# RNN lead of 52 steps instead of 64, set-up placed by RNN step, and eight matmuls without a result per RNN-only step

## The chip, the cores and the metric

The kernel runs on one core of a Trainium2 chip. The metric is the device time of one execution in microseconds (us). Five engines share the work: TensorE (PE, with its weight loads shown as PEld), VectorE (DVE), ScalarE (ACT), GpSimd (POOL) and SyncE (SP, which here only issues DMAs).

## The reference

A sequence of 4 batches, 1024 tokens and width 512 in float32 goes through four residual layers. Two of them are recurrences over the tokens, so that their steps can't run in parallel. The condition (4 x 512) is the start state of both, and the input of the last layer's small network.

```python
# layer 0: RNN, started from cond
h_t = tanh(x_t @ Wx + b + h_{t-1} @ Wh);           x1 = x + h
# layer 1: conv over 4 tokens (taps from cond), then a diagonal scan of 64 states
proj = conv(x1) @ Wp + bp;  B = softplus(proj[:64]);  C = tanh(proj[64:])
u = x1 @ Ws + bs;  s_t = decay * s_{t-1} + dt * B_t * u_t;  x2 = x1 + (C * s) @ Wo + bo
# layer 2: LSTM, started from cond, gates i, f, o, g
A = x2_t @ Wx + b + h_{t-1} @ Wh
c_t = sig(f) * c_{t-1} + sig(i) * tanh(g);  h_t = sig(o) * tanh(c_t);   x3 = x2 + h
# layer 3: per batch a 512 x 512 matrix, made once from cond
hid = gelu(layernorm(cond) @ w1 + b1);  a, b = split(hid @ w2 + b2)    # w2 is 512 x 8192
out = x3 + x3 @ (base + a @ b^T)
```

## The kernel before

**Passes and steps.** The tokens are cut into 32 chunks of 32 steps. The program is one list of steps, written out in full: `do_pass(c)` writes 32 of them, in which the LSTM works on chunk c and the RNN on a chunk that lies ahead. The RNN leads by two chunks: passes -2 and -1 (64 steps) have no LSTM in them and are the set-up phase, passes 0 to 29 have both, and passes 30 and 31 have the LSTM alone. Each engine executes its own instructions in the order in which the program writes them.

**One LSTM step.** TensorE runs 96 bf16 matmuls (`lstm_mm`, L360; h is split into three bf16 parts), in an order in which the four blocks of half A (gates of h units 0 to 255) end before the last block of half B. For each half, VectorE transposes the sums out of PSUM (L377), adds the parts and the input (L382), ScalarE takes tanh of the gates (L389), VectorE makes products (L393) and cell (L398), ScalarE tanh of the cell (L403), VectorE h (L406) and the two further splits of h (L187, twice). Then the next step's 96 matmuls can start. The RNN step beside it is 16 float32 matmuls (`rnn_mm`, L335), a transpose (L343), an addition (L344), both on VectorE, and a tanh on ScalarE (`rnn_h`, L347).

**Jobs.** All other work of a pass is a list of jobs, each with a slot (the step t of the pass) and a place in that step: "pe" (TensorE, between the LSTM's and the RNN's matmuls), "gap" (after half B's cell, before its tanh) or "end" (after `rnn_h`). Where several have one slot and place, they stand in the order of the list. The jobs are

- `project0` (L290, L304): the RNN's input of chunk c+3, four "pe" jobs;
- `ssm_jobs`: layer 1 of chunk c+1: x1 = x + h (L424), `taps` in four "pe" jobs and `skip` in one (L290, L457 to L472 for what follows), the scan (L475), a copy of the last state `s1` on ScalarE (L465), the product `y` on VectorE in place over the scan's result (L480), `out_mm` (L290) and `x2_end` (L492);
- `input_jobs`: the LSTM's input of chunk c+1 in four groups of 8 tokens: `input_mm` (L316, four "pe" jobs for each group), `input_turn` (L320, VectorE), `input_bias` (L328, ScalarE);
- `adapt_jobs`: layer 3 of chunk c-1: four additions (L666), four "pe" jobs (L673), a copy of 128x512 out of PSUM on ScalarE (L680), and DMAs to the output.

**Set-up.** The dictionary `early` holds what is done once, by pass and step: `split_wh2` (L274 to L279, 16 pieces; the LSTM's weights are split into three bf16 parts), `prepare_decay`, `fold_conv` (L255, L259), the layer norm (L526 to L547), `adapt_hidden` (L558), 32 `adapt_w2` (L575: 16 matmuls on 1/32 of w2, copies at L581, and the load of a further 512 KB of w2 into one of four buffers), `adapt_gather` (L589, POOL's DMAs), `adapt_sum` (L610), `base_identity` (L624) and 16 `adapt_layer` (L615 two matmuls, L616 an addition of 128x512). In this kernel all 32 `adapt_w2` stand in passes -1 and 0, one for each step from step 3 of pass -1, and the `adapt_layer` stand in pass 0. The identity `ident` is made on POOL, behind the DMAs that POOL issues at the start.

Of the kernel before, what the change touches and what calls it, by code (L numbers as in the profile page):

```python
# [20 lines left out]
TG = 8  # L21
CT = 32
# [15 lines left out]
def cond_resid_kernel(ctx: ExitStack, tc: tile.TileContext, a: dict, out: bass.AP):  # L38

# [135 lines left out]
    def load_late():  # L175
        quads(nc.sync, w1, a["w1"].rearrange("(j c q) n -> j q c n", j=4, c=KC))
        for j in range(W2_BUFS):
            load_w2(j)
        quads(nc.sync, base, a["base"].rearrange("(j c q) n -> j q c n", j=4, c=KC))
# [63 lines left out]
    def prepare_decay():  # L243
        for f in softplus_parts(sp, vec[:NS, 2:4], 2, "p"):
            f()
        nc.vector.tensor_mul(dec1, sp[:, 0:1], dt)
        nc.vector.tensor_scalar(dec1, dec1, -1.0, 1.0, ALU.mult, ALU.add)
        nc.vector.tensor_copy(decay, dec1.to_broadcast([NS, TC]))
# [12 lines left out]
    b2s = const.tile([P, 4, KC], F32, name="b2s", tag="b2s")  # L261

    def scale_b2():
        nc.vector.tensor_scalar(b2s[:, 0:3], b2[:, 0:3], 0.5, None, ALU.mult)
        nc.vector.tensor_copy(b2s[:, 3], b2[:, 3])

    def split_wh2(k, g):

        w, scale, cols = layer[:, k, g], 0.5 if g == 3 else 0.25, slice(g * D, (g + 1) * D)
        part = [x[:, k, cols] for x in wh2]  # L270
        left = xw2[1][:, 2 + g % 2].rearrange("p c t b -> p (c t b)")

        def first():
            nc.scalar.activation(part[0], upper(w), AF.Copy, scale=scale)  # L274
            nc.vector.scalar_tensor_tensor(left, w, scale, part[0], ALU.mult, ALU.subtract)

        def second():
            nc.scalar.copy(part[1], upper(left))
            nc.vector.tensor_tensor(part[2], left, part[1], ALU.subtract)  # L279

        return first, second
# [43 lines left out]
    def input_bias(c, n, g, m):  # L325

        x = xw2[c % 2][:, g, m, TG * n : TG * (n + 2), :]
        nc.scalar.activation(x, x, AF.Identity, bias=b2s[:, g, m : m + 1], scale=1.0 if g == 3 else 0.5)  # L328


    def rnn_mm(c, t):
        h = h0[c % 2] if t else h0[(c - 1) % 2]
        for k in range(KC):
            for j in range(4):
                nc.tensor.matmul(  # L335
                    acc0[CT * j : CT * j + B, :],
                    h[:, k, (t - 1) % TC, :], wh0[:, k, j * P : (j + 1) * P],
                    start=(k == 0), stop=(k == KC - 1),
                )

# [27 lines left out]
    class Half:  # L368
# [19 lines left out]
        def gates(self):  # L388
            nc.scalar.activation(self.gc[:, :4], self.gc[:, :4], AF.Tanh)  # L389
# [26 lines left out]
    def ssm_jobs(c):  # L416
# [3 lines left out]
        def sm(name):  # L420
            return small.tile([NS, TOK], F32, name=name, tag=name, bufs=1)

        jobs = [
            (m // 2, ("gap", "end")[m % 2], lambda m=m: v.tensor_add(x1[:, m, 3:, :], x[:, m], h[:, m]))  # L424
            for m in range(KC)
# [22 lines left out]
        jobs += [(1 + k, "pe", lambda k=k: taps(k)) for k in range(KC)]  # L448
        jobs.append((5, "pe", skip))

        def turn(n):
# [5 lines left out]
            (4, "end", lambda: act.activation(z, pb[:NS, 0, :], AF.Identity, bias=vec[:NS, 0:1])),  # L457
            (4, "end", lambda: act.activation(e, pb[:NS, 0, :], AF.Abs, bias=vec[:NS, 0:1])),
            (5, "end", lambda: act.activation(e, e, AF.Exp, scale=-1.0)),
            (5, "end", lambda: act.activation(u, e, AF.Copy, bias=2.0)),  # L460
            (6, "end", lambda: act.activation(cg, pb[NS:, 0, :], AF.Tanh, bias=vec[NS:, 0:1])),
            (7, "end", lambda: v.tensor_mul(u, u, e)),
            (7, "end", lambda: v.tensor_mul(w, u, u)),
            (7, "end", lambda: act.activation(p, w, AF.Copy, scale=2.0 * SERIES[-1])),
            (12, "end", lambda: act.copy(s1, y_last)),  # L465
# [17 lines left out]
        jobs += [(6 + n // 3, place(n), lambda n=n: turn(n)) for n in range(4)]  # L483
        jobs += [(8 + n // 3, place(n), f) for n, f in enumerate(chain)]
# [6 lines left out]
        def x2_end(m):  # L491
# [6 lines left out]
            (13, "pe", out_mm),  # L498
            *((13 + m // 2, "end", lambda m=m: x2_end(m)) for m in range(KC)),
            (14, "end", lambda: act.copy(x1[:, :, 0:3, :], x1[:, :, TC : TC + 3, :])),  # L500
# [4 lines left out]
    hid = prep.tile([P, KC, B], F32, name="hid", tag="hid")  # L505
# [45 lines left out]
    def adapt_hidden():  # L551
# [12 lines left out]
        nc.vector.tensor_add(hid, tt[:, :, :B], bm1.unsqueeze(2).to_broadcast([P, KC, B]))  # L564
        nc.scalar.activation(hid, hid, AF.Gelu)

    def adapt_w2(j):
# [4 lines left out]
        for k in range(KC):  # L572
            for t in range(4):
                n0 = P // 2 * (t % 2)
                nc.tensor.matmul(  # L575
                    ps[CT * t : CT * t + B, :], hid[:, k, :], w2[j][:, t // 2, k, n0 : n0 + P // 2],
                    start=(k == 0), stop=(k == KC - 1),
                )
        for t in range(4):
            copy = (nc.vector.tensor_copy, nc.scalar.copy)[t % 2]  # L580
            copy(xr[CT * t : CT * t + B, half, hd, rg], ps[CT * t : CT * t + B, :])  # L581
# [36 lines left out]
    def base_identity():  # L618
# [11 lines left out]
    early = {  # L630
        (-2, 9): [prepare_decay], (-2, 12): [scale_b2], (-2, 24): [fold_conv], (-2, 26): [adapt_center], (-2, 28): [adapt_norm],
        (-1, 2): [adapt_hidden], (-1, 20): [base_identity],
    }
# [3 lines left out]

    late = None
    for n in range(4 * KC):
        first, second = split_wh2((1, 0, 2, 3)[n // 4], n % 4)  # L640
        t = 4 + 3 * n // 2
        if late:
            at(-2, t, late)
        at(-2, t, first)
        late = second
    at(-2, 29, late)
    at(-2, 30, load_late)

    for half in range(2):
        at(-1, half, lambda half=half: adapt_bias(half))  # L650
        at(0, 7, lambda half=half: adapt_sum(half))
    for j in range(NW2):
        c, t = divmod(3 + j, TC)
        at(c - 1, t, lambda j=j: adapt_w2(j))
        if j % (NW2 // 2) == NW2 // 2 - 1:
            at(c - 1, t, lambda half=j // (NW2 // 2): adapt_gather(half))
    for n in range(B * KC):
        at(0, 8 + 3 * n // 2, lambda n=n: adapt_layer(n // KC, n % KC))


    def adapt_jobs(c, dst):
# [22 lines left out]
        jobs = [(2 + m, "end", lambda m=m: add(m)) for m in range(KC)]  # L684
        jobs += [(6 + k, "pe", lambda k=k: mm(k)) for k in range(KC)]
        return jobs + [(5 + KC, "end", end)]


    def input_jobs(c):
        jobs = []  # L690
        for n in range(TC // TG):

            ps = bank("proj2", [P, D], tag=("po", "ada")[n % 2], bufs=1)
            t = 15 + KC * n
            jobs += [(t + k, "pe", lambda n=n, k=k, ps=ps: input_mm(c, n, k, ps)) for k in range(KC)]
            jobs += [
                (t + KC - 1 + g // 2, "end", lambda n=n, g=g, ps=ps: input_turn(c, n, g, ps)) for g in (0, 2)
            ]
        jobs += [
            (23 + (KC * g + m) // 2, "end", lambda g=g, m=m: input_bias(c, 0, g, m))  # L700
            for g in range(4) for m in range(KC)
        ]
        return jobs

    def late_jobs(c):
        return [
            ((KC * g + m) // 2, "end", lambda g=g, m=m: input_bias(c, 2, g, m))
            for g in range(4) for m in range(KC)
        ]


    def do_pass(c, src=None, dst=None, lstm=True, rnn=True, ssm=True, late=True, last=False):

        jobs = []
        if dst is not None:
            jobs += adapt_jobs(c - 1, dst)
        if ssm:
            jobs += ssm_jobs(c + 1)
        if src is not None:
            jobs.append((2, "end", lambda: load_x(c + 4, src)))  # L720
        if rnn and c + 3 < NCHUNK:
            for m in range(KC):
                mm, end = project0(c + 3, m)
                t = ((0, 10, 11, 12) if lstm else (8, 10, 12, 14))[m]
                jobs += [(t, "pe", mm), (t, "end", end)]
        if ssm:
            jobs += input_jobs(c + 1)
        if late:
            jobs += late_jobs(c)
# [6 lines left out]
        for t in range(TC):  # L736
# [8 lines left out]
            if rnn:  # L745
                rnn_mm(c + 2, t)
# [16 lines left out]
            if lstm:  # L763
                if not (last and t == TC - 1):
# [6 lines left out]
            if rnn:  # L771
                rnn_pre(c + 2, t)
                rnn_h(c + 2, t)
            do(t, "end")
            for f in early.pop((c, t), ()) if dst is None else ():
# [7 lines left out]
    do_pass(-2, lstm=False, ssm=False, late=False)  # L783
    do_pass(-1, src=a["xT"][3], lstm=False, late=False)
    for m in range(2):
        lstm_input(0, 0, m)
    do_pass(0, src=a["xT"][4])
    assert not early
    prep_ctx.close()

# [3 lines left out]
    for c in range(1, NCHUNK):  # L794
        do_pass(
            c, src=a["xT"][c + 4] if c + 4 < NCHUNK else None, dst=dst(c - 1), rnn=c + 2 < NCHUNK,
            ssm=c + 1 < NCHUNK, last=c + 1 == NCHUNK,
        )
# [60 lines left out]
```

## Time and profile before

| | |
|---|---|
| median of 3 runs | 4811.99 us (4811.18 to 4814.89) |
| the profiled execution's own time | 4806.8 us |
| its span, first to last instruction | 4805.0 us |
| PE busy | 4609.9 us, 96% |
| DVE busy | 3816.7 us, 79% |
| ACT busy | 1749.1 us, 36% |
| first transpose of the RNN / of the LSTM | 18.6 us / 192.4 us from the span's start |

A row of the profile gives the line of the kernel, the engine, the operation with its operands and their shapes, how often it ran, the busy time, the mean of one, and what ended the idle time before it. Line numbers are those of the kernel before. In a timeline a row starts with its start and its length in us. PEclk is the clock that TensorE was granted, as a share of full speed.

### The profile page before, as it was taken

The page shows a single profiled execution, that of the slowest core. Times are in us where ns is not written, and L with a number is a line of the kernel's source. Part 1 is how long each engine was busy: PE and PEld are TensorE (multiplying, and loading weights), DVE is VectorE, ACT ScalarE, POOL GpSimd, SP SyncE. Part 2 cuts the span into 40 slices and gives each one's busy share as a digit, 9 for nine tenths or more (in the row PEclk, how much of TensorE's full clock was granted, in tenths as well). Part 3 has the DMA queues.
Part 4 walks back from the last instruction along what each step waited for, and adds up shares of the span by engine and source line. Part 5 has one row for each costly group of instructions (what it writes and reads, how often), then busy time and mean ns, then how long its engine had stood idle before and what let it go on. Part 6 is the DMA issues. An engine that isn't in the chain of part 4 may idle for free.

```text
span 4805.0 us, 321617 instructions
## 1 busy us (share of the span) xinstructions
PE 4609.9 (96%) x147040; PEld 3529.9 (73%) x147040; DVE 3816.7 (79%) x17843; ACT 1749.1 (36%) x8712; POOL 52.1 (1%) x95
## 2 busy tenths in 40 slices
PE   6899999999999999999999999999999999999876
PEld 4777777777777777777777777777777777777654
DVE  3678888888888888888888888888888878888776
ACT  2333333333333333333333333333333333333332
POOL 2100000000000000000000000000000000000000
PEclk7999999999999999999999999999999999999999
DMA  6400000000000000000000000000000000000000
GB/s 138 130 4 9 9 9 9 7 7 9 9 9 9 7 8 7 9 9 9 7 9 7 9 9 9 7 9 6 9 9 9 9 7 6 9 7 6 6 3 7
DMA packets 38787, 67.47 MB, mean 14 GB/s; under 512 B 9056, under 2 KB 26080, under 8 KB 36400
## 3 DMA queue, kind: packets, MB, share of 16 engines
q1 hardware_dynamic: 34064, 46.68, 3.8%
q8 instruction: 1149, 18.83, 1.7%
q14 instruction: 214, 1.75, 0.1%
q0 software_dynamic: 2208, 0.19, 0.1%
q10 hardware_dynamic: 1152, 0.01, 0.0%
HBM read 38.34 MB, written 8.39 MB: 10 GB/s over the span
## 4 chain that ended last, share of the span: by engine, by line
PE 94%; DVE 5%; issue 1%; ACT 0%; DMA 0%; ACTq 0%; DVEq 0%; SPq 0%
PE acc L360 58%; PE acc L335 18%; PE proj L316 9%; PE pb L290 3%; PE proj L290 2%; PE ada L673 2%; DVE tt L377 1%; DVE gc L382 1%; DVE h L187 1%; PE ssm_out L290 1%; DVE h L406 1%; DVE prod L393 0%; DVE gc L398 0%; PE pl L615 0%; PE pp L575 0%
## 5 line engine op out<-in xcount | busy, mean ns | idle before, releaser
L360 PE MATMUL acc<-wh,h 128*12 128x256 bf16 x98304 | 2875.0, 273 | 134.7 <-DVE h L187 130.0
L360 PEld LDWEIGHTS <-h 128*12 128x12 bf16 x98304 | 2266.7, 87 | 693.9 <-DVE h L187 372.3
L377 DVE STREAM_TRANSPOSE tt<-acc 128x256 f32<-128x256 f32 x2048 | 922.0, 450 | 425.5 <-PE acc L360 305.6
L335 PEld LDWEIGHTS acc<-wh,h 128*4 128x4 f32 x32768 | 815.6, 88 | 521.3 <-issue 212.2
L335 PE MATMUL acc<-wh,h 128*4 128x128 f32 x32768 | 1109.1, 276 | 31.6 <-ACT h L347 27.8
L389 ACT ACTIVATE gc<-gc 128x32 f32<-128x32 f32 x2048 | 469.7, 229 | 1038.6 <-DVE gc L382 948.4
L382 DVE TENSOR_REDUCE gc<-tt 128x32 f32<-128x128 f32 x2048 | 777.1, 379 | 35.3
L187 DVE TENSOR_TENSOR h<-h 128x8 f32<-128x8 f32 (+1 forms) x4098 | 681.1, 166 | 104.7
L403 ACT ACTIVATE th<-gc 128x8 f32<-128x8 f32 x2048 | 427.2, 209 | 831.9 <-DVE gc L398 831.9
L347 ACT ACTIVATE h<-pre 128x16 f32<-128x16 f32 x1024 | 221.4, 216 | 1144.7 <-DVE pre L344 1144.7
L316 PE MATMUL proj<-wx,x 128*32 128x512 f32 x4096 | 529.5, 592 | 2.6 <-issue 1.5
L406 DVE SCALAR_TENSOR_TENSOR h<-gc,th 128x8 f32<-128x8 f32 x2048 | 343.1, 168 | 221.8 <-ACT th L403 205.1
L343 DVE STREAM_TRANSPOSE tt<-acc 128x128 f32<-128x128 f32 x1024 | 316.2, 309 | 70.3 <-PE acc L335 70.1
L398 DVE SCALAR_TENSOR_TENSOR gc<-prod 128x8 f32<-128x8 f32 x2048 | 341.9, 167 | 35.5
L366 ACT COPY tt<-xw 128x32 f32<-128x32 f32 x2048 | 327.9, 207 | 0.0
L393 DVE SCALAR_TENSOR_TENSOR prod<-gc 128x16 f32<-128x16 f32 x2048 | 315.3, 154 | 0.0
L328 ACT ACTIVATE xw<-xw,b2s 128x64 f32<-128x64 f32 x1024 | 293.6, 334 | 0.4
L344 DVE TENSOR_TENSOR pre<-xw,tt 128x16 f32<-128x16 f32 x1024 | 179.8, 176 | 37.4
L290 PE MATMUL proj<-xin,wx 128*32 128x128 f32 x4096 | 138.8, 278 | 11.9 <-DMA wx<-in_Wx_dram 11.8
L290 PE MATMUL pb<-x,wp 128*32 128x128 f32 x4096 | 139.5, 274 | 0.1
L673 PE MATMUL ada<-layer,x 128*32 128x512 f32 x1024 | 131.6, 592 | 3.0 <-DVE x L666 3.0
L290 PEld LDWEIGHTS proj<-xin,wx 128*32 128x32 f32 x4096 | 117.1, 112 | 14.0 <-DMA wh<-in_Wh_dram 11.8
(116 smaller groups left out, 1179.0 us busy)
## 6 DMA issues: line engine op xcount, KB each, us to landing
layer<-in_w2T_dram SPq DMA_DIRECT2D x32, 512.0 KB, 4.1
xin<-in_xT_dram SPq DMA_DIRECT2D x128, 64.0 KB, 2.1
out_dram<-x SPq DMA_DIRECT2D x128, 64.0 KB, 1.8
layer<-in_Wh_dram SPq DMA_DIRECT2D x16, 256.0 KB, 9.7
wx<-in_Wx_dram SPq DMA_DIRECT2D x4, 1024.0 KB, 15.5
wx<-in_Wx_dram SPq DMA_DIRECT2D x4, 256.0 KB, 5.2
wh<-in_Wh_dram SPq DMA_DIRECT2D x4, 256.0 KB, 7.9
layer<-in_w_dram SPq DMA_DIRECT2D x4, 256.0 KB, 23.7
```

The costliest lines, as they stand in the source:

```text
L187: nc.vector.tensor_tensor(h[:, :, n], h[:, :, n - 1], upper(h[:, :, n - 1]), ALU.subtract)
L290: nc.tensor.matmul(dst[CT * j : CT * (j + 1)], columns(j), x, start=first, stop=final)
L316: nc.tensor.matmul(ps[CT * j : CT * (j + 1), :], tok, w[:, j], start=(k == 0), stop=(k == KC - 1))
L335: nc.tensor.matmul(acc0[CT * j : CT * j + B, :], h[:, k, (t - 1) % TC, :], wh0[:, k, j * P : (j + 1) * P], start=(k == 0), stop=(k == KC - 1),
L360: nc.tensor.matmul(acc2[mh][CT * j : CT * j + NP * B, :], parts, w[:, :, n0 : n0 + 2 * CT], start=(k == 0 and n == 0), stop=(k == KC - 1 a ...
L366: nc.scalar.copy(tt2[m][t % 2][:, :, :, :B], xw2[c % 2][:, :, 2 * m : 2 * m + 2, t, :])
L377: nc.vector.transpose(self.tt[:, :, :, B:].rearrange("p g c b -> p (g c) b"), acc2[self.m])
L382: nc.vector.tensor_reduce(self.gc[:, :4].rearrange("p g c b -> p (g c) b"), self.tt[:, :, :, : (1 + NP) * B].rearrange("p g c (s b) -> p ( ...
L389: nc.scalar.activation(self.gc[:, :4], self.gc[:, :4], AF.Tanh)
L398: nc.vector.scalar_tensor_tensor(self.c, self.prod[:, 1], 0.5, self.prod[:, 0], ALU.mult, ALU.add)
L403: nc.scalar.activation(self.th, self.c, AF.Tanh, scale=0.5)
L406: nc.vector.scalar_tensor_tensor(self.out[:, :, 0], self.gc[:, 2], 1.0, self.th, ALU.add, ALU.mult)
```

## The change

The RNN leads by `LEAD = 52` steps, so that the set-up phase has 52 RNN steps (20 in pass -2, 32 in pass -1), and the RNN ends at step 11 of pass 30. Layer 1 of a chunk therefore starts in slot 9 of the pass before it, and nearly every job moves to another slot. The LSTM's input of a chunk is made for 8 tokens in the pass before and for the other 24 in the pass itself. The input's bias moves from ScalarE (32 instructions of 128x64 in a pass) to VectorE (8 of 128x256); the factor 0.5 that went with it is now in the gates' tanh, and the g part of the weights and the bias is doubled in the set-up. The set-up is placed by RNN step (`at_step`); 12 of the 32 `adapt_w2` stand in it, and 20 in steps 0 to 19 of pass 0; the `adapt_layer` stand in steps 25 to 31 of pass 0 and 0 to 8 of pass 1. `adapt_w2` multiplies with 32 columns instead of 4 and needs one copy instead of four. In steps 0 to 24 of the passes without LSTM, `keep_busy` issues eight bf16 matmuls of 128x256 with `ident` as both operands, whose result nobody reads.

```diff
+LEAD = TC + 20
...
-    def input_bias(c, n, g, m):
-        x = xw2[c % 2][:, g, m, TG * n : TG * (n + 2), :]
-        nc.scalar.activation(x, x, AF.Identity, bias=b2s[:, g, m : m + 1], scale=1.0 if g == 3 else 0.5)
+    def input_bias(c, n, g):
+        x = xw2[c % 2][:, g : g + 2, :, TG * n : TG * (n + 1), :].rearrange("p g c t b -> p g c (t b)")
+        nc.vector.tensor_add(x, x, b2[:, g : g + 2].unsqueeze(3).to_broadcast([P, 2, KC, TG * B]))
...
+    bits = ident.bitcast(BF16)
+    idle = bank("idle", [P, 2 * P], tag="ada", bufs=1)
+    def keep_busy():
+        for n in range(2):
+            for j in range(4):
+                nc.tensor.matmul(idle[CT * j : CT * (j + 1), :], bits[:, :CT], bits, start=True, stop=True)
...
-            (m // 2, ("gap", "end")[m % 2], lambda m=m: v.tensor_add(x1[:, m, 3:, :], x[:, m], h[:, m]))
-            for m in range(KC)
+            (9, "end", lambda: add(slice(0, 2), 0, TC - 4)),
+            (10, "gap", lambda: add(slice(2, 4), 0, TC - 4)),
+            (11, "end", lambda: add(slice(0, 4), TC - 4, TC)),
...
-        jobs += [(1 + k, "pe", lambda k=k: taps(k)) for k in range(KC)]
-        jobs.append((5, "pe", skip))
+        jobs += [(12 + k, "pe", lambda k=k: taps(k)) for k in range(KC)]
+        jobs.append((16, "pe", skip))
...
-            (12, "end", lambda: act.copy(s1, y_last)),
+            (23, "end", lambda: act.copy(s1, y_last)),
...
-        jobs += [(8 + n // 3, place(n), f) for n, f in enumerate(chain)]
+        jobs += [(19 + n // 3, place(n), f) for n, f in enumerate(chain)]
...
-            (13, "pe", out_mm),
-            *((13 + m // 2, "end", lambda m=m: x2_end(m)) for m in range(KC)),
+            (24, "pe", out_mm),
+            *((24 + (m + 1) // 2, ("end", "gap")[m % 2], lambda m=m: x2_end(m)) for m in range(KC)),
...
-        for t in range(4):
-            copy = (nc.vector.tensor_copy, nc.scalar.copy)[t % 2]
-            copy(xr[CT * t : CT * t + B, half, hd, rg], ps[CT * t : CT * t + B, :])
+        nc.scalar.copy(xr[:, half, hd, rg], ps)
...
+    def at_step(i, f):
+        c, t = divmod(i - LEAD, TC)
+        at(c, t, f)
+    for n, f in enumerate(decay_parts()):
+        at_step(1 + n // 2, f)
...
+            at_step(5 + n, first)
...
+    at_step(10, load_w1)
+    for j in range(W2_BUFS):
+        at_step((14, 18)[j // 2], lambda j=j: load_w2(j))
+    at_step(21, load_base)
+    at_step(20, fold_conv)
...
+    at_step(24, adapt_center)
+    at_step(25, adapt_norm)
...
+    at_step(30, adapt_hidden)
+    NPRE = 12
     for j in range(NW2):
...
+        if j < NPRE:
+            at_step(32 + 3 * j // 2, f)
+        else:
+            at(0, j - NPRE, f)
...
+    for half in range(2):
+        at(0, 24, lambda half=half: adapt_sum(half))
+    at(0, 23, base_identity)
     for n in range(B * KC):
-        at(0, 8 + 3 * n // 2, lambda n=n: adapt_layer(n // KC, n % KC))
+        c, t = divmod(25 + n, TC)
+        at(c, t, lambda n=n: adapt_layer(n % B, n // B))
...
-        jobs = [(2 + m, "end", lambda m=m: add(m)) for m in range(KC)]
-        jobs += [(6 + k, "pe", lambda k=k: mm(k)) for k in range(KC)]
-        return jobs + [(5 + KC, "end", end)]
+        jobs = [((1, 2, 5, 6)[m], "end", lambda m=m: add(m)) for m in range(KC)]
+        jobs += [((16, 21, 22, 23)[k], "pe", lambda k=k: mm(k)) for k in range(KC)]
+        return jobs + [(23, "end", end)]
...
+    def input_jobs(c, n, t):
...
+        last = t + KC - 1
+        return [(t + k, "pe", lambda k=k: mm(k)) for k in range(KC)] + [
+            (last, "end", lambda: input_turn(c, n, 0, ps[0])),
+            (last + 1, "gap", lambda: input_turn(c, n, 2, ps[0])),
+            (last + 1, "end", lambda: input_bias(c, n, 0)),
+            (last + 2, "gap", lambda: input_bias(c, n, 2)),
+        ]
...
+        if -1 <= c < NCHUNK - 1:
+            jobs += ssm_jobs(c + 1)
+            jobs += input_jobs(c + 1, 0, 25)
         if src is not None:
-            jobs.append((2, "end", lambda: load_x(c + 4, src)))
+            jobs.append((12, "end", lambda: load_x(c + 4, src)))
+        if c + 3 < NCHUNK:
             for m in range(KC):
                 mm, end = project0(c + 3, m)
+                jobs += [(17 + m, "pe", mm), (17 + m, "end", end)]
+        if lstm:
+            for n in range(1, TC // TG):
+                jobs += input_jobs(c, n, KC * (n - 1))
...
             if rnn:
-                rnn_mm(c + 2, t)
+                rnn_mm(*r)
+            if not lstm and t < 25:
+                keep_busy()
```

## The prediction

> **What bounds the kernel now.** I read the busy time and clock in stretches first, then the timeline of single steps, then the waits, and the chain of waits for what ended each step. The stretches (length, busy time and instructions of each engine, clock, DMA share, GB/s) are two of the set-up and one of the passes with LSTM and RNN:
>
> ```profile
> 57.00:84.00 27.00, 18.79 (x320) 10.12 (x320) 13.38 (x32) 9.57 (x25) 0.00 (x0) 0.50 0.72 177
> 150.00:190.00 40.00, 36.77 (x1183) 26.35 (x1187) 18.93 (x88) 14.18 (x66) 9.09 (x16) 1.00 0.67 216
> 2000.00:2143.00 143.00, 141.34 (x4560) 108.53 (x4560) 117.18 (x551) 53.43 (x269) 0.00 (x0) 1.00 0.03 8
> ```
>
> From 57 to 112 us the clock is halved. There an RNN step takes 2.78 us (in the chain its matmuls start at 59.92, 62.71, 65.49, each 1.93 long); the first RNN steps, at full clock, took 2.02. The LSTM's first matmul comes at 190.5 us, so the set-up is 4% of the time.
>
> One LSTM step, and the start of the next, in pass 14 (timeline, rows of other work left out):
>
> ```profile
> 2273.40 2.79 PE L360 MATMUL acc<-wh,h 128*12 128x256 bf16 x96
> ...
> 2274.57 0.18 DVE L344 TENSOR_TENSOR pre<-xw,tt 128x16 f32<-128x16 f32 x1
> ...
> 2275.26 0.45 DVE L377 STREAM_TRANSPOSE tt<-acc 128x256 f32<-128x256 f32 x1
> ...
> 2276.02 1.05 PE L290 MATMUL proj<-xin,wx 128*32 128x128 f32 x32
> ...
> 2276.89 1.05 PE L335 MATMUL acc<-wh,h 128*4 128x128 f32 x32
> ...
> 2277.86 2.36 PE L360 MATMUL acc<-wh,h 128*12 128x256 bf16 x80
> ...
> 2279.25 0.22 ACT L347 ACTIVATE h<-pre 128x16 f32<-128x16 f32 x1 [1.07 <-DVE pre L344]
> 2279.37 0.18 ACT L465 COPY s<-w 64x4 f32<-64x4 f32 x1
> ...
> 2279.58 0.34 DVE L480 SCALAR_TENSOR_TENSOR w<-w,sp,cg 64x128 f32<-64x128 f32 x1 [0.37 <-ACT s L465]
> 2279.85 0.43 DVE L377 STREAM_TRANSPOSE tt<-acc 128x256 f32<-128x256 f32 x1
> ```
>
> From start to start TensorE spends 2.62 us on the LSTM, 0.87 on one "pe" job and 0.97 on the RNN (0.87 where nothing holds it, as in the set-up): 4.46 a step. In pass 31, without RNN and without most jobs, transposes are 4.45 apart too. So a step has **two limits of nearly one length**: the recurrence through DVE and ACT at 4.455, and PE with one job at 2.62+0.86+0.87 = 4.35. Half A's transpose starts 1.87 us after the first matmul. What VectorE still does then delays it: in slot 12's "end" job `y` waits 0.37 for ScalarE's copy of `s1`, the transpose comes 1.99 after its matmuls, and that step takes 4.61 in the median pass. Slots 15 to 31 are at 4.45 to 4.47. Passes 1 to 31 lie 22 us in all over 31 x 142.56, pass 0 lies 20 over.
>
> Three prices for later. `skip` (0.77 from start to start) and an `adapt_jobs` matmul group (0.85), in the order of PE alone:
>
> ```profile
> 3101.99 0.93 PE L290 MATMUL pb<-x,ws 128*32 128x128 f32 x14
> ...
> 3106.45 1.03 PE L673 MATMUL ada<-layer,x 128*32 128x512 f32 x8
> 3107.30 0.94 PE L335 MATMUL acc<-wh,h 128*4 128x128 f32 x28
> ```
>
> And POOL's making of `ident`, held up behind the small loads on its queue:
>
> ```profile
> 32.31 0.29 POOL masks.py:199 TENSOR_SCALAR_AFFINE_SELECT ident<-ident 128x128 f32<-128x128 f32 x1
> ```
>
> **What the Trainium skill says.** "TensorE: Matmul & The Clock Gate", Part 1, has a clock that activity raises to full and that falls to half after an idle window of about 3.4 us. The two values agree (1.00 and 0.50), the condition doesn't: here it fell at 29.9 us after six RNN steps with no matmul gap over 0.97 us, so a low share is enough. Its section on the 16 sub-arrays says that ScalarE and VectorE work strictly in order and that TensorE only pulls weight loads ahead; the 0.37 us wait above is such a case. "VectorE: DVE Perf Modes", on Mode 2×_2P, keeps fp32 tensor_tensor at one element per cycle, 0.96 GHz: 1.04 ns. The trace: 287 ns for 128x128 (L424), 176 for 128x16 (L344), so 0.99 ns.
>
> **The change, part by part.**
>
> *Set-up.* (a) `keep_busy` stands behind the first `rnn_mm` and needs `ident`, ready at 32.6 us. PE's queue is stopped from 18.5 to 32.6, and the second RNN step, at 19.5 before, starts at about 33: **13.5 us lost**. (b) Eight such matmuls cost 8/96 of 2.62 = 0.22 us, in the 1.1 us in which PE waits for tanh: nothing on the path while that cover lasts. Worth of the clock: at half clock, three groups of 32 matmuls in a window of 6.8 us brought it back (43.6 to 50.4), 2.5 (RNN alone) didn't; with 0.44 us more each I take it back at 43.6. (c) Steps: 1 to 4 at 2.78, to 44; 5 to 20 with a split each, bound by VectorE (0.69+0.69 and the waits for two ACT copies of 0.6): 2.52 warm, 2.78 cold; steps 13 to 19 have no `keep_busy` and turn cold: to 83. 20 to 31: 2.05 to 2.8 each, with `fold_conv`, layer norm, hidden layer and their table loads (1.28 each) some 8 us more: to 117. 32 to 44: RNN 0.87 and a PE remainder of 0.22+0.87+0.45 (`adapt_w2`) in two steps of three: 2.3 each, to 147. 45 to 51: 2.1, to 162. The LSTM starts at about 163 instead of 190.5: **-27**. Always warm: 154 (-36); cold to step 31: 178 (-12).
>
> *DMA and queues.* SP's order stays (x, weights, w1, w2, base), and 4 x 512 KB in six steps (14 us, 150 GB/s) is under the 216 seen. POOL gets one memset more, after `ident`. No gain or loss here.
>
> *Passes 0 and 1.* 20 `adapt_w2` of 0.45 beside a full step: 2.62+0.86+0.87+0.45 = 4.80, +0.35 each: 7. Their 16 loads of w2 disturb PE's instruction fetch: the 28 loads of before cost about 7 us of "issue" in the set-up, so 4 (0 to 10). `base_identity` (16 x 0.12) and `adapt_sum` (2 x 0.6) before transposes: 3. `adapt_layer` 1.05 in 13 full slots and three free ones: 13.7+1. Sum 29, against about 21 before: **+8** (3 to 18).
>
> *Steady passes.* Three collisions, each against 4.455:
> - Slot 16 has `skip` and an `adapt_jobs` group: 2.62+0.85+0.77+0.87 = 5.11, **+0.66**. The RNN's tanh and everything in the next step wait behind it.
> - Slot 23 "end": in ACT's order the 128x512 copy (0.585, about 0.49 to the next start) now stands before the copy of `s1`. `y` then starts 2.20 after the matmuls instead of 1.72, and the transpose at 2.49: **+0.50** on what it costs now.
> - Slot 11 "end": the addition of the last four tokens needs the tanh of the same step. The tanh ends 1.60 after the matmuls, the addition takes 0.22, the `input_turn` behind it 0.37 to the next start: transpose at 2.15, **+0.28**.
>
> Elsewhere: `input_bias` on VectorE, 0.287+128x0.00099 = 0.41 (0.35 to the next start), and `input_turn` (0.37) in "gap", where VectorE has 0.36 before half B's h: +0.01 each, below which nothing is seen; if full lengths count, 0.1 in nine slots. ScalarE's 293.6 us of bias were idle-time work: nothing. `out_mm`'s long step is hidden behind slot 23: -0.07. Loads of x move to slot 12 with their fetch stalls, and the outputs to a step with slack: -0.1. Sum 1.27 a pass; 29 passes have slots 16 and 23 with RNN: **+37** (22 to 58).
>
> *Sum.* -27+8+37 = **+18** on 4806.8. The median of the runs shown lies 5.2 above this execution: 4812+18 = **4830**.
>
> **Rivals.** (A) As summed, 4830: 0.44. (B) The clock stays low through the set-up: -12 instead of -27, 4845; for it, that a PE 70% busy (18.79 of 27.00) was left at half clock: 0.16. (C) The gap doesn't hold turn and bias: nine slots of 0.1 in 29 passes, +26, 4856; against it, reciprocals of 0.32 cost nothing in "gap": 0.12. (D) Faster: the collisions vanish because queues run apart enough to absorb them, so that only -27+8 is left: 4793. It decides where the three collisions together cost under 0.3 a pass (9 us). Against it, 0.12 us at the transpose is already visible in slot 12: 0.12. (E) Both halves cancel, with the set-up at -36 and the collisions at two thirds (+25): 4809; also where `keep_busy` isn't stopped by `ident`: 0.16.
>
> **Numbers.** A measurement here can tell 0.2% (9.6 us) from no change. Slower is A, B, C: 0.72; same E: 0.16; faster D: 0.12. The range leaves out D and the outer half of C: 4803 to 4857.
>
> **What would show it.** Right: PE idle from 18.5 to 32.6 with the wait on POOL; LSTM from about 163 us; steps of 5.1 in slot 16; `y` waiting about 0.85 behind ACT; a full clock from about 44 us with a dip. Wrong: steps near 4.46 in slots 11, 16 and 23, an LSTM start after 175 or before 152, or transposes late in slots 4, 8 and 12.

## The result and the profile after

The changed kernel takes 4839.9 us (median of 5 runs, 4838.52 to 4843.03), the kernel before 4811.99 (4811.18 to 4814.89): a ratio of 1.0063, interval 1.0051 to 1.0075. It is slower by 27.9 us, three times what can be told from no change. The profiled execution of after has 4843.03 us with a span of 4841.2; against the 4805.0 of before that is 36.2 more, 8 more than the medians differ, because the execution of before was 5.2 below its median and the one of after 3.1 above.

I cut both spans into stretches (us); the first ends with the LSTM's first matmul, and a pass is counted from its first transpose of half A to that of the next pass:

| stretch | before | after | difference | predicted |
|---|---|---|---|---|
| start to the LSTM's first matmul | 190.5 | 176.0 | -14.5 | -27 |
| passes 0 and 1 | 162.9 + 144.7 | 172.0 + 154.4 | +18.8 | +8, and +1.3 of pass 1's collisions |
| passes 2 to 30 | 4154.7 | 4185.4 | +30.7 | +36 |
| pass 31 and tail | 150.3 | 150.3 | 0 | 0 |

(The LSTM's first transpose comes 1.9 us after its first matmul in before and 3.1 in after, where the clock is halved from 175.1 to 178.6 us; this is the 1.2 us that the rows leave.) All three signs are those of the prediction; each size is off.

**Stretches of after** (length, busy time and instructions of PE, PEld, DVE, ACT, POOL, clock, DMA share, GB/s):

```profile
57.00:84.00 27.00, 14.28 (x328) 9.09 (x320) 16.14 (x41) 11.64 (x29) 0.00 (x0) 0.79 0.55 140
...
2000.00:2143.00 143.00, 140.28 (x4529) 108.82 (x4525) 117.97 (x555) 45.57 (x236) 0.00 (x0) 1.00 0.03 8
```

The clock of the first stretch rose from 0.50 to 0.79, but in the same 27 us the number of matmuls hardly changed (320 to 328), of which some now have no result. In the steady stretch PE is busy 1.06 us less of 143 and does 31 matmuls fewer: it waits. ACT's busy time fell by 7.9 us and shortened nothing.

**The start of after's set-up** (timeline, rows of PE and the row of POOL that ends the wait):

```profile
30.82 0.29 POOL masks.py:199 TENSOR_SCALAR_AFFINE_SELECT ident<-ident 128x128 f32<-128x128 f32 x1
31.17 0.62 PE L350 MATMUL idle<-ident 128*32 128x256 bf16 x8 [13.50 <-POOL ident masks.py:199]
...
42.09 0.52 PE L292 MATMUL proj<-xin,wx 128*32 128x128 f32 x10 [1.43 <-issue]
...
51.58 1.71 PE L292 MATMUL proj<-xin,wx 128*32 128x128 f32 x26 [5.56 <-issue]
...
60.79 0.28 PE L337 MATMUL acc<-wh,h 128*4 128x128 f32 x2 [3.54 <-issue]
```

The bracket is the idle time ahead of a row and what ended it. The first wait is the predicted one: 13.50 us for `ident`. The other three, 10.5 us in all, end with "issue": no semaphore that the profile shows held PE, and the prediction had none of them here (before has 2.1 us of them on PE between 17 and 110 us).

The DMA packets of the trace show what ends these waits. The profile calls two of its DMA queues "instruction"; a packet of 16 KB on one of them ended at 40.63, 49.94 and 59.33 us, and PE went on at 42.09, 51.58 and 60.79, each time 1.5 to 1.6 us later. In pass 0 of the twelve traces here (about 40 such packets each), all 148 "issue" waits of PE end 1.1 to 1.7 us after one. By these times, what PE waits for is its instructions.

**Slot 16 of after** in pass 14, with `skip` and an `adapt_jobs` group between the LSTM's matmuls and the RNN's:

```profile
2307.81 2.80 PE L371 MATMUL acc<-wh,h 128*12 128x256 bf16 x96
...
2310.43 1.03 PE L711 MATMUL ada<-layer,x 128*32 128x512 f32 x8
2311.29 0.93 PE L292 MATMUL pb<-x,ws 128*32 128x128 f32 x14
2312.07 1.03 PE L337 MATMUL acc<-wh,h 128*4 128x128 f32 x28
2312.83 0.28 PE L371 MATMUL acc<-wh,h 128*12 128x256 bf16 x2
...
2314.90 0.45 DVE L388 STREAM_TRANSPOSE tt<-acc 128x256 f32<-128x256 f32 x1 [1.09 <-PE acc L371]
```

From 2307.81 to 2312.83 are 5.02 us, also the median over the passes; slot 17 takes 4.66. PE goes from group to group without a gap, and VectorE waits 1.09 us for it. The first two matmuls of slot 17 are recorded ahead of the RNN's last, so that the sum of the two steps, 9.68 (8.91 in before), is surer than its split.

**Slot 23 of after** in pass 14 (the answer to the step shown of before, where this stood in slot 12):

```profile
2344.39 2.79 PE L371 MATMUL acc<-wh,h 128*12 128x256 bf16 x96
...
2345.94 0.59 ACT L718 COPY x<-ada 128x512 f32<-128x512 f32 x1
...
2346.42 0.19 ACT L482 COPY s<-w 64x4 f32<-64x4 f32 x1
...
2346.64 0.34 DVE L497 SCALAR_TENSOR_TENSOR w<-w,sp,cg 64x128 f32<-64x128 f32 x1 [0.90 <-ACT s L482]
2346.91 0.43 DVE L388 STREAM_TRANSPOSE tt<-acc 128x256 f32<-128x256 f32 x1
...
2349.32 2.80 PE L371 MATMUL acc<-wh,h 128*12 128x256 bf16 x96
```

The copy of 128x512 stands ahead of the copy of `s1` on ScalarE, `y` waits 0.90 instead of 0.37, the transpose starts 2.52 us after the matmuls, and the step, which is step 24, takes 4.93.

### The profile page after: what moved, and what is told of

It reads as the page before. It is cut to its first block, busy times and chain, and to the rows that moved or that the text cites. A ratio compares the mean times of both kernels' runs of the same rounds, so it can differ in the third digit from the quotient of the medians.

```text
span 4841.2 us, 321327 instructions
## 1 busy us (share of the span) xinstructions
PE 4615.9 (95%) x147344; PEld 3550.6 (73%) x147344; DVE 3865.2 (80%) x18001; ACT 1495.0 (31%) x7661; POOL 52.6 (1%) x96
## 4 chain that ended last, share of the span: by engine, by line
PE 89%; DVE 8%; issue 1%; ACT 1%; DMA 0%; POOL 0%; ACTq 0%; DVEq 0%; POOLq 0%
PE acc L371 56%; PE acc L337 16%; PE proj L318 9%; PE pb L292 3%; PE proj L292 2%; DVE tt L388 2%; PE ada L711 2%; DVE gc L393 1%; DVE h L191 1%; DVE h L417 1%; DVE prod L404 1%; DVE gc L409 1%; DVE tt L354 0%; ACT x L718 0%; PE pl L633 0%
## 5 line engine op out<-in xcount | busy, mean ns | idle before, releaser
L318 PEld LDWEIGHTS proj<-wx,x 128*32 128x32 f32 x4096 | 118.2, 110 | 6.0 <-PE pp L595 0.6
```

Of the source, the lines that this page charges most:

```text
L318: nc.tensor.matmul(ps[CT * j : CT * (j + 1), :], tok, w[:, j], start=(k == 0), stop=(k == KC - 1))
```

## Experiments

The theory: three separate costs (slot 16, slot 23, `ident` ahead of the second RNN step) and a dearer pass 0 make the result, and a gain from the shorter set-up stands against them. The rivals: the queues absorb the collisions; the matmuls without a result, and not the stop, decide the set-up; the loads of w2, and not the added PE work, decide pass 0. Ratios are to the kernel before on the same chip. The start of the LSTM is good to some 6 us only: four kernels with one and the same set-up (after, E1, E2, E5; "the four equals" below) have it at 176.0, 172.6, 175.0 and 170.2. Pass 0 varies too: in five kernels with one and the same program for it (after, E2, E3, E8, E4) it takes 172.0, 170.6, 171.1, 171.9 and 166.6. Of E4's difference 1.7 us are the clock's, as shown below.

**E1, `skip` alone in its slot.**

```diff
-        jobs.append((16, "pe", skip))
+        jobs.append((17, "pe", skip))
...
-                jobs += [(17 + m, "pe", mm), (17 + m, "end", end)]
+                t = (18, 19, 20, 29)[m]
+                jobs += [(t, "pe", mm), (t, "end", end)]
```

> The changed kernel with skip in slot 17, alone on TensorE there, and project0 in slots 18, 19, 20 and 29 instead of 17 to 20. Nothing else moves. If the two TensorE jobs in slot 16 are the cost, slot 16 (5.02 us in the median pass) and slot 17 (4.66) both go back to 4.46, which is 29 times 0.66 to 0.78: 19 to 23 us less than the changed kernel's 4840, so about 4819. If those steps are long because of the loads of x that slot 12 now starts and PE's instruction fetch beside them, the time stays within 5 us of 4840.

Measured: 4812.19 us, ratio 1.0006 (0.9999 to 1.0013), level with before. In pass 14, on PE:

```profile
2294.10 1.03 PE L711 MATMUL ada<-layer,x 128*32 128x512 f32 x8
2294.96 1.05 PE L337 MATMUL acc<-wh,h 128*4 128x128 f32 x32
2295.93 2.79 PE L371 MATMUL acc<-wh,h 128*12 128x256 bf16 x96
2298.55 0.93 PE L292 MATMUL pb<-x,ws 128*32 128x128 f32 x14
```

The two groups now stand in two steps, and slots 16 and 17 take 4.46 in the median, against 5.02 and 4.66. Passes 2 to 30 are 22.0 us shorter; 28 x (0.57+0.21) is 21.8 (pass 30 has no RNN in these slots). So the one step with two "pe" jobs is most of the loss of the steady passes, and the queues absorb none of it. The other 7 us of the spans' difference lie in the set-up (3.4, inside the spread named above) and mostly in passes 0 and 1.

**E2, the copy of `s1` ahead of the copy of 128x512.**

```diff
-        return jobs + [(23, "end", end)]
+        return jobs + [(24, "end", end)]
```

> The changed kernel with layer 3's copy out of PSUM and its output DMAs in slot 24 instead of 23, so that ScalarE copies s1 first. If the copy ahead of s1 is what makes the step after slot 23 last 4.93 us, y waits 0.37 us again instead of 0.85 and that step takes 4.60: 29 times 0.33, 9 to 10 us less, about 4830. If out_mm on TensorE holds that step anyway, under 3 us are gained.

Measured: 4825.25 us, 1.0036 (1.0023 to 1.0049); passes 2 to 30 are 13.2 us shorter. Pass 14:

```profile
2334.45 2.79 PE L371 MATMUL acc<-wh,h 128*12 128x256 bf16 x96
...
2336.16 0.34 DVE L497 SCALAR_TENSOR_TENSOR w<-w,sp,cg 64x128 f32<-64x128 f32 x1 [0.37 <-ACT s L482]
2336.43 0.43 DVE L388 STREAM_TRANSPOSE tt<-acc 128x256 f32<-128x256 f32 x1
2337.17 1.08 PE L292 MATMUL ssm_out<-w,wo 64*32 64x128 f32 x32
2338.18 1.06 PE L337 MATMUL acc<-wh,h 128*4 128x128 f32 x32
2339.05 2.80 PE L371 MATMUL acc<-wh,h 128*12 128x256 bf16 x96
```

The wait of `y` is 0.37 again and the step takes 4.60, as before. So ScalarE's order is the cause: 4.93-4.61, 28 times, is 9.0 us. Of the other 4, 3 lie in slot 16, which the edit doesn't touch: its mean was 5.14 in after and 5.04 here, by steps in which PE waits longer for "issue". The lines show more: PE goes from one group to the next without a gap (2.72 to `out_mm`, 1.01 for it, 0.87 for the RNN, 4.60 in all). What makes this step long is `out_mm`, not the transpose at 1.98.

**E3, no `keep_busy`.**

```diff
-            if not lstm and t < 25:
-                keep_busy()
```

> The changed kernel without the matmuls that have no result. If the stop for the identity is the larger part, the second RNN step starts at about 19.5 us instead of 31.6, the clock stays low for more steps, and the LSTM starts at 158 to 165 us instead of 176: 4822 to 4829. If the clock that they hold is worth what the stop costs, the LSTM starts near 176 and the time stays at 4836 to 4844. If it is worth more, it is later and slower than 4844.

Measured: 4823.36 us, 1.0029 (1.0017 to 1.0041), faster than after. The LSTM starts at 161.9, the second RNN step at 19.6 instead of 31.6, where it now waits for the first step's tanh alone:

```profile
19.61 1.06 PE L337 MATMUL acc<-wh,h 128*4 128x128 f32 x32 [0.96 <-ACT h L358]
```

Until 110 us the clock is halved for 65 us in all, most of it from 48 to 102.

**E4, `keep_busy` with an operand that is there.** The bf16 parts are taken from a weight tile instead of from `ident`.

```diff
-    bits = ident.bitcast(BF16)
+    bits = upper(wx0[:, 0])[:, : 2 * P]
```

> The changed kernel with the upper halves of the RNN's first input weights as the operands of the matmuls without a result; these have landed before the first RNN step, so that nothing waits for the identity. If the stop and the clock are separate effects, the LSTM starts 13 us earlier than in the changed kernel, at 163 us, and the time is about 4827, below that of the kernel without these matmuls. If the instruction fetch stalls between 40 and 61 us are what holds the early steps, they come at the same time and the gain is under 5 us.

Measured: 4823.53 us, 1.0027 (1.0015 to 1.0038); the LSTM starts at 158.8, and the clock is halved for 41 us in all, most of it from 56 to 83. The second RNN step with its matmuls without a result:

```profile
18.74 1.06 PE L337 MATMUL acc<-wh,h 128*4 128x128 f32 x32 [0.73 <-ACT h L358]
19.61 0.41 PE L350 MATMUL idle<-wx 128*32 128x256 bf16 x8
```

The stop is gone, and the LSTM starts 11 to 17 us earlier than in the four equals, about what the stop was worth. Against E3 the clock is full for 24 us more, the LSTM starts 3 us earlier, which is within the spread, and the medians are equal. So in the set-up `keep_busy` costs through its operand, and its use for the clock is 3 us or less.

**E5, no late loads of w2.** The last 16 loads are left out (the last 16 `adapt_w2` read the same four buffers again).

```diff
-            load_w2(j + W2_BUFS)
+            if j + W2_BUFS < 16:
+                load_w2(j + W2_BUFS)
+            else:
+                w2[j + W2_BUFS] = w2[j]
```

> The changed kernel without the last 16 of the 32 loads of w2, which are those issued in pass 0; the matmuls on them run on what lies in the buffers, so layer 3's matrix is left out in part. All matmuls and copies stay. If the loads disturb PE's instruction fetch, pass 0 (172.0 us in the changed kernel) loses 8 to 14 us and the time is near 4829. If the 20 groups of matmuls in full steps are the whole cost of that pass, it loses under 3.

Measured: 4832.38 us, 1.0057 (1.0040 to 1.0074); pass 0 is 167.3 instead of 172.0. PE's waits in pass 0, in us, times and longest: first after, then this kernel.

```profile
PE acc L371 <- issue: 3.9, 7, 0.7
PE pp L595 <- issue: 3.8, 6, 0.9
...
```

```profile
PE acc L371 <- issue: 3.6, 7, 0.7
PE pp L595 <- issue: 0.7, 1, 0.7
```

What the loads cost isn't settled. Pass 0 is 4.7 us shorter than in after and 3.3 shorter than in E2, but E4, which has all the loads, has 166.6, or 168.3 with the clock's 1.7 us. The "issue" waits fall to 4.3 us from after's 8.6 (which holds 0.9 on `skip`'s and `taps`' line); the other kernels with all the loads have 4.6 to 8.4. One execution of each kernel can't tell this from the spread, and the ratio is after's within the intervals. What is shown is that waits of 4.3 us stay without these loads, so that they are not the only cause, and that the 8 to 14 us of the first theory are not there.

**E6, 20 of the 32 `adapt_w2` in the set-up.**

```diff
-    NPRE = 12
+    NPRE = 20
...
-            at_step(32 + 3 * j // 2, f)
+            at_step(32 + j, f)
...
-            at(0, j - NPRE, lambda half=j // (NW2 // 2): adapt_gather(half))
+            f = lambda half=j // (NW2 // 2): adapt_gather(half)
+            at_step(32 + j, f) if j < NPRE else at(0, j - NPRE, f)
```

> The changed kernel with 20 of the 32 pieces of w2 in the set-up, one for each RNN step from step 32, and 12 in pass 0 instead of 20. If a piece costs pass 0 the 0.35 us of its matmuls and 0.5 us or so of fetch stalls, pass 0 gets some 6 us shorter, the set-up 2 to 3 longer, and the time is 4836 to 4838. If 512 KB for each step of 2.2 us is more than the DMA engines give, the LSTM starts later by more than pass 0 gains, and the time is 4840 or above.

Measured: 4834.05 us, 1.0058 (1.0043 to 1.0073). Pass 0 falls by 8.7 us to 163.3; the LSTM starts at 177.9, later by 1.9 than in after and by up to 7.7 than in its equals. The whole is 0.05% under after, which the intervals don't tell from nothing: inconclusive as a mend. Against the kernels named above, E4 apart, pass 0 is 7.3 to 8.7 us shorter, so the eight steps had cost 0.9 to 1.1 each there, not the 0.55 of the prediction (7+4 for 20 steps).

**E7, the edits of E1, E2 and E4 together.**

```diff
-    bits = ident.bitcast(BF16)
+    bits = upper(wx0[:, 0])[:, : 2 * P]
...
-        jobs.append((16, "pe", skip))
+        jobs.append((17, "pe", skip))
...
-        return jobs + [(23, "end", end)]
+        return jobs + [(24, "end", end)]
...
-                jobs += [(17 + m, "pe", mm), (17 + m, "end", end)]
+                t = (18, 19, 20, 29)[m]
+                jobs += [(t, "pe", mm), (t, "end", end)]
```

> Skip in slot 17, layer 3's copy in slot 24, and the early operand, all three in the changed kernel. If they are separate, their ratios to the kernel before (1.0006, 1.0036 and 1.0027 against 1.0063) add up to 0.0057+0.0027+0.0036 less: 0.994, 4785 us on 4812, faster than both kernels. If slots 16 and 23 or the set-up hide one another, less than 45 of these 55 us come off, and it is 4795 or above.

Measured: 4784.39 us, 0.9958 (0.9943 to 0.9973), faster than before. From after's 1.0063 that is 0.0105, about 50 us; the three edits alone gave 0.0057, 0.0027 and 0.0036, together 0.0120. Within the intervals they add, so they are separate causes. Passes 2 to 30 take 4146.9, 7.8 less than before the change; the LSTM starts 32.6 us earlier than there, and passes 0 and 1 take 15 more.

**E8, Wx2 loaded later.** The "issue" waits of the set-up stand beside the load of 4 MB of Wx2; here its four DMAs are issued in RNN step 10.

```diff
-    wx2 = load_rows(const, "wx2", a["Wx2"], 4 * D, nc.sync)
+    wx2 = const.tile([P, KC, 4 * D], F32, name="wx2", tag="wx2")
...
+    def load_wx2():
+        quads(nc.sync, wx2, a["Wx2"].rearrange("(j c q) n -> j q c n", j=4, c=KC))
...
+    at_step(10, load_wx2)
```

> The changed kernel with the 4 MB load of the LSTM's input weights moved behind that of w1, which waits for the first splits (RNN step 9), so that it doesn't run beside RNN steps 5 to 8. If this load is what holds up PE's instruction fetch there (10.5 us of issue waits between 40 and 61 us), those steps take 2.1 to 2.8 us and the LSTM starts about 8 us earlier: 4832. If the stalls follow the load to the later steps, or come from the first fetch of new instructions whatever the DMA does, the LSTM starts near 176 and the time stays at 4840.

Measured: 4832.68 us, 1.0056 (1.0041 to 1.0071). The LSTM starts at 165.7, below the four equals. PE's waits between 17 and 110 us:

```profile
PE idle L353 <- POOL ident masks.py:199: 13.0, 1, 13.0
PE proj L295 <- issue: 1.9, 1, 1.9
```

The stop stays, the "issue" waits fall from 10.5 us (8.4 to 10.5 in the four equals) to 1.9; the ratio alone can't be told from after's. So these steps wait where the load runs beside them. The load alone is not enough: here it runs from 56 to 82 us, beside RNN steps without a "pe" job, and none of these waits for "issue"; steps 5 to 8 have `project0` besides, and with it twice the matmuls. How the load delays the packets of instructions was not tested; the DMA engines move both.

**E9, E7 and E8 together.**

```diff
-    wx2 = load_rows(const, "wx2", a["Wx2"], 4 * D, nc.sync)
+    wx2 = const.tile([P, KC, 4 * D], F32, name="wx2", tag="wx2")
...
-    bits = ident.bitcast(BF16)
+    bits = upper(wx0[:, 0])[:, : 2 * P]
...
+    at_step(10, load_wx2)
```

> The three edits of the run before (skip in slot 17, layer 3's copy in slot 24, early operand) and the later load of the LSTM's input weights. Alone, that load took the LSTM's start from 176.2 to 165.7 us. If the stalls of early steps are the same ones with an early operand (steps of 5.1, 3.8 and 6.4 us after the fifth), the LSTM starts at about 149 us instead of 157.9 and the ratio to the kernel before is 0.994, about 9 us below the three edits together. If the load now meets other work of the set-up, the start stays within 3 us of 158.

Measured: 4783.69 us, 0.9952 (0.9940 to 0.9965), no better than E7 within the intervals. The waits came back:

```profile
PE acc L340 <- issue: 6.5, 3, 4.1
```

Without the stop, steps 5 to 7 run at 27 to 42 us, beside the load that comes first, Wh2 (also 4 MB, landed at 40.3). In after and E8 the stop kept these steps out of that time. The gain of E8 holds for its own order of things only.

**E10, E9 with the edit of E6.**

```diff
-    NPRE = 12
+    NPRE = 20
...
-            at_step(32 + 3 * j // 2, f)
+            at_step(32 + j, f)
...
+            at_step(32 + j, f) if j < NPRE else at(0, j - NPRE, f)
```

> The four edits and 20 of the 32 pieces of w2 in the set-up. In the changed kernel this made pass 0 8.7 us shorter (172.0 to 163.3) and the LSTM's start 1.7 us later, 7 us in all by the spans, though the ratios of the timed runs were only 0.0005 apart. If the spans say right, it is 5 to 7 us below the four edits; if the loads of w2 come too late in the shorter set-up, it is level with them or above.

Measured: 4781.27 us, 0.9947 (0.9933 to 0.9960): the lowest of all, 0.5% under before, not told apart from E9. Pass 0 is at 162.2, as in before, and the LSTM starts at 160.5, 30 us earlier than in before. So the shorter lead and the new placement of the set-up bring a gain once the three costs are taken out.

## Why the prediction was right, and where not

The side and the time (4830 for 4839.9) were right, the time in part by luck. The sum was made on the profiled execution and said +18; the two profiled executions differ by 36.2, the medians by 27.9. The set-up was 12.5 us and passes 0 and 1 were 9.5 us too low, the steady passes 5 too high. One of the prediction's own signs of being wrong came true, an LSTM start after 175 us (176.0), and rival B's numbers (4845, a start at 178) lie nearer to the result than A's. Its cause, a low clock, is not what held the set-up.

- **Stop at `ident`: right.** PE stands for 13.50 us. The 13.5 predicted were the delay of the second RNN step, which is 12.1 (31.6 for 19.5), so that the equal digits are chance; the first step, up to the start of the second, takes 15.0 us instead of 2.0 (13.3 to 15.5 in the four equals). E3 and E4 take the stop away.
- **Set-up, -27: mis-sized, -14.5** (-14.5 to -20.3 in the four equals). Two terms of step (c) failed. The steps were counted without "issue" waits, which are 10.5 us here, most of the 12.5 that are missing; E8 ties them to the 4 MB load. And the full clock "from 44 with a dip" did not come: it changed between 0.5 and 1.0 eight times from 35 to 117 us (mean 0.79 in the stretch above). So what was said of rival B, a low clock, is half true, but E3 and E4 show how little hung on it: most of these steps wait for VectorE and ScalarE. (b), eight matmuls that cost nothing in PE's wait, holds where they don't stop.
- **Passes 0 and 1, +8: mis-sized, +18.8.** The `adapt_layer` steps cost the predicted 1.05, and undisturbed `adapt_w2` steps the predicted 4.80. The failed term is "4 (0 to 10)" for the disturbed fetch: 8.6 us of "issue" in pass 0 (1.5 in before's). The recorded idle time is not all of their cost, as step 3 shows:

```profile
191.21 0.63 PE L595 MATMUL pp<-layer,hid 128*32 128x64 f32 x32
191.65 2.83 PE L371 MATMUL acc<-wh,h 128*12 128x256 bf16 x96
...
196.00 0.40 PE L595 MATMUL pp<-layer,hid 128*32 128x64 f32 x15
197.34 0.47 PE L595 MATMUL pp<-layer,hid 128*32 128x64 f32 x17 [0.94 <-issue]
197.59 2.68 PE L371 MATMUL acc<-wh,h 128*12 128x256 bf16 x90
```

  The undisturbed group gives way to the next after 0.44 us, the disturbed one after 1.59: 1.15 lost, 0.94 recorded, because a matmul's recorded end lies past the start of the next. At 0.2 or a little more for each of the 15 waits, they cost about 12 us, three times the term. That the loads of w2 are their cause, as the prediction had it, was not shown (E5). With 1.25 us for step 0, where the clock is halved, this accounts for steps 0 to 21 (21.2 us over 4.455 each, 7 of them for the matmuls, as predicted) to within about 1 us.
- **`base_identity` and `adapt_sum`, 3: right, and a term was missing.** Step 24 takes 7.53, 3.1 more than 4.455. PE waits 2.74 us for it, and step 25 then takes 7.17 instead of the 5.51 of a step with `adapt_layer`. The clock explains this 1.7. First after's matmuls of step 25 with its clock beside them, then the same step of E4, where the clock stays full:

```profile
311.64 4.46 PE L371 MATMUL acc<-wh,h 128*12 128x256 bf16 x96 [2.74 <-DVE h L191]
...
311.70:315.10 3.40, 3.40 (x68) 2.35 (x72) 2.42 (x9) 0.42 (x2) 0.00 (x0) 0.50 0.00 0
```

```profile
289.46 2.80 PE L371 MATMUL acc<-wh,h 128*12 128x256 bf16 x96 [2.75 <-DVE h L191]
```

  In E4 and E9, the two traces with the full clock here, step 25 takes 5.51; in the nine other traces of changed kernels 6.8 to 7.2.
- **Slot 16, +0.66: right in mechanism, a little small.** +0.57 in its own step and +0.21 in the next: 0.78. E1 confirms it.
- **Slot 23, +0.50: mechanism and time of the transpose right, cost too high.** Predicted `y` at 2.20 and transpose at 2.49, measured 2.25 and 2.52; but the step costs 4.93, 0.32 more than its 4.61 before.
- **Slot 11, +0.28: too high.** Transpose at 2.14 (predicted 2.15), cost 0.08 in step 12.
- The last two share one failed step: the delay of half A's transpose was counted in full. A delay of 0.27 cost 0.08, one of 0.65 cost 0.47, so about 0.19 is free. VectorE's rows of after in pass 14 show where it is, first a step without delay (slot 19), then step 24:

```profile
2323.81 0.45 DVE L388 STREAM_TRANSPOSE tt<-acc 128x256 f32<-128x256 f32 x1
...
2324.79 0.45 DVE L388 STREAM_TRANSPOSE tt<-acc 128x256 f32<-128x256 f32 x1
```

```profile
2346.91 0.43 DVE L388 STREAM_TRANSPOSE tt<-acc 128x256 f32<-128x256 f32 x1
...
2347.68 0.43 DVE L388 STREAM_TRANSPOSE tt<-acc 128x256 f32<-128x256 f32 x1
```

  Half B's transpose follows half A's by 0.98 in the first, where it waits for the last of the 96 matmuls, and by 0.77 in the second, where these have long ended. The 0.21 is given back there. The reading of before that led to counting in full was wrong too: its 4.61 in slot 12 was put down to a transpose at 1.99, inside what is free, and E2 shows PE without a gap through `out_mm`.
- **Turn and bias in the gap: right.** Slots 4, 5, 8, 9, 13, 29 and 30 take 4.45 to 4.46 (slot 12 takes 4.54, behind the addition of slot 11), so rival C fell. The bias costs its own length only, and that was right (0.41 predicted):

```profile
L330 DVE TENSOR_TENSOR xw<-xw,b 128x256 f32<-128x256 f32 x256 | 107.0, 418 | 0.2 <-issue 0.2
```

- **Steady sum:** predicted 1.27 a pass, 36 us in passes 2 to 30; measured 30.7. Summed over these passes by slot, slots 16 and 17 bring +25.2 us, step 24 less the long step that before had in slot 13 +7.0, step 12 +1.2. The -0.1 a pass for the loads of x and the outputs failed: slots 3 to 5, behind before's loads, lose 8.3 us, and slots 15 and 19 to 21, behind after's, gain the same 8.3. The rest is -2.7.
- **Rival D** (queues absorb the collisions) needed under 0.3 a pass and fell. What E7, E9 and E10 show is its time by another way: with the collisions moved away, not absorbed.

## What to carry to other kernels

Where two engines are each near the limit of a step, count what every engine issues in each step, not in each pass: one slot with two groups of matmuls and one long copy ahead of a short one on a queue in strict order cost more here (31 us) than the shorter lead saved (14.5). Before a delay is charged in full, look at what must be waited for anyway beyond it. Filler work must depend on nothing that is late, or it stops the queue that it was to keep running.

## What was not expected of the hardware

- PE's clock falls under a load that is far from idle: in before, RNN steps with PE busy about half the time (1.06 of 2.02 us) lose the full clock. Eight more short matmuls in each step do not hold it where the steps take 2.8 us: in E8 it falls at 54.7 us, with `keep_busy` in every step and no "issue" wait since 41.7.
- The clock changes in stretches of 3.4 us or a multiple. In the first 420 us of the twelve traces PE's recorded busy share in the last 3.4 us was 0.62 or less ahead of each of the 70 falls, and 0.76 or more ahead of each of the 70 rises; no stretch of 3.4 us at full clock with a share under 0.44 went without a fall after it. So a single wait of 2.7 us (step 24) can cost the next 3.4 us half their speed.
- PE waits for "issue" up to 5.6 us at once beside a load of 4 MB (E8: at most 1.9 with the load elsewhere), and still 4.3 us in pass 0 without the loads of w2 (E5). Such a wait ends 1.1 to 1.7 us after a 16 KB packet of the queue called "instruction" (148 of 148 in pass 0), and it costs some 0.2 us more than the idle time that the profile records.
- The same set-up differs by 6 us between executions, and the same pass 0 by up to 5, so a gain there of a few us can be seen in the waits at most, but not in the time.
